# Layer 3's shifted copies in a four-layer convolution kernel: ScalarE copies replaced by DMAs that ScalarE issues

## The chip, the cores and the metric

The kernel runs on one core of a Trainium2 chip. A core has five engines that each work through their own list of instructions in order: PE (TensorE, matrix products), DVE (VectorE), ACT (ScalarE), POOL (GpSimd) and SP (SyncE, which here only issues DMAs). They meet through semaphores. Beside them 16 DMA engines move data between the memories; SP, ACT and POOL can issue DMAs. The metric is the time of one execution on the device in microseconds (us), the median of several runs. The profile is of one execution; its span runs from the first to the last instruction.

## The reference

The input `x` is 16 images of 64 channels of 128 by 128 pixels in float32. Four layers follow each other, each of the form x = x + layer(group_norm(x)):

```python
x = x + _L0_conv_ref(_gn(x), ...)   # channel Gram matrix of the image, then a 1x1 convolution
x = x + _L1_conv_ref(_gn(x))        # |Sobel x| + |Sobel y| in each channel
x = x + _L2_conv_ref(_gn(x), ...)   # shift of some channels by a column, 3x3 convolution, 64 -> 64 channels
x = x + _L3_conv_ref(_gn(x), ...)   # 3x3 convolution, 1x1 convolution, batch norm, leaky ReLU, clip to 0..255
```

`_gn` is a group norm over pairs of channels of one image. The batch norm of layer 3 takes its mean and variance over all 16 images, so the end of layer 3 (normalize, clip, add) can start only when the last image's convolution is done.

## The kernel before, in words

**Tiling.** A tile holds 128 partitions: 64 channels times two rows (or two halves of the image), and along the free axis four pairs of rows of 128 pixels. An image has `NS = 8` chunks of this kind. Products go to PSUM tiles of 512 numbers in each partition.

**The 3x3 convolutions of layers 2 and 3.** Two neighbouring rows of output, `s = 0` and `s = 1`, share rows of input, and a difference of input rows serves in place of some products. `difference(name, n, t)` writes on DVE the difference of two rows into the tile `d2` or `d3`, half `n` of 0 and 1. Each of these tiles is allocated once, 128 partitions by 2 halves by 4 rows by 130 columns, a zero column on either side. `shared(...)` is the product common to both output rows (into a tile `one`), `own(...)` that of one row (into `two`).

**The twins.** For one half of the output channels only one of the two row blocks of the difference is needed, 64 of the 128 partitions. For these the kernel keeps a second tile, `qd2` and `qd3`, called the twin: in one half of its partitions it holds the difference as it is, in the other half the same difference shifted by a column. One product over 128 partitions then serves two columns of the 3x3 kernel (weights `pk`). `own` reads it:

```python
some[o] = [
    (p[cols(o), 0:m], pk, q[:, :, 1:1 + W]),
    (p[cols(o), 0:m, 0:W - 1], wt[:, n, 2, cols(o)], d[:, :, 2:1 + W]),
]
```

`twin(n)` makes the twin of half `n`, in two copies of 64 partitions each. In layer 2 (`Layer2.twin`) POOL issues two DMAs for it. In layer 3 (`Layer3.twin`) ACT makes two copies.

**Order of the work.** The program is a chain of steps (the loop at the end of the kernel), each of four quarters `q = 0..3`. In every step four stages are at work on different images or chunks: Gram (loads `xr`, layer 0's Gram matrix), Front (layer 0's mix and layer 1, from loads `x`; result `u` stored to `x_d`), Layer2 (loads `v` from `x_d`, normalizes them on ACT, result stored to `x_d` again as layer 3's input), and Layer3 (reads layer 2's result from SBUF, writes `y` and stores it to `y_d`). Layer3 runs ten steps behind Layer2, so it is alone in the last steps. Layer 3's part of a step is: at `q = 0` the twin of half 1, the shared product and the product of row 0 (which uses half 0); at `q = 1` the product of row 1 (half 1), the bias `c` on ACT, the normalization of the next chunk, and the stores of the last chunk's `y`; at `q = 2` the sum `y` on DVE and the difference of half 0 for the next step; at `q = 3` the twin of half 0, the difference of half 1, and the squares of `y` on ACT. Layer 2 loads `v` of the chunk after next at `q = 1`, and normalizes the next chunk's `v` there.

The class `InOrder` keeps every engine's instructions in the order in which the program names them. DMAs issued by SP and ACT signal that they have landed by one of eight semaphores, taken in rotation in program order, and a DMA waits until the one that held its semaphore before has landed. POOL's DMAs have eight of their own. Waits between engines, and between a buffer's reader and its next writer, are set by the framework.

**After the last step** the tiles of the earlier stages are used as room for the end: `y_d` and `x_d` are read back, normalized by ACT (ReLU with scale and bias), clipped and added by DVE, and stored.

In the profile nearly all instructions have one line, that of the helper class, so it is read by tiles (`qd<-d`: into a twin from a difference; tile numbers are left out, so `d` and `qd` stand for layers 2 and 3, and `x_d` for the stored results of layers 1 and 2 alike).

Of the kernel before, what the change touches and what calls it, by code (L numbers as in the profile page):

```python
# [15 lines left out]
B, C, H, W = 16, 64, 128, 128  # L16
# [7 lines left out]
CP = 4  # L24
# [20 lines left out]
def single(table, n):  # L45

    for o in range(2):
        planes = [i for m, i, half, _ in table if (m, half) == (n, o)]
        if len(planes) == 1:
            return o, planes[0]  # L50
# [58 lines left out]
def tile_kernel(ctx: ExitStack, tc: tile.TileContext, x, cw_h, w2_t, b2, wbin_t, w1_t, b1, gamma, beta, consts, out):  # L109
    nc = tc.nc  # L110
    pe, dve, act, sp, pool = (InOrder(tc, e) for e in (nc.tensor, nc.vector, nc.scalar, nc.sync, nc.gpsimd))
# [24 lines left out]
    def flat(ap):  # L136
        return ap.rearrange("p j w -> p (j w)")
# [28 lines left out]
    def cols(o):  # L166
        return slice(o * C, (o + 1) * C)
# [568 lines left out]
    class Layer2:  # L736
# [42 lines left out]
        def twin(self, n):  # L779

            d, q = diffs["d2"], twins["d2"]
            _, i = single(TO_SLOTS, n)
            pool.dma_start(flat(q[cols(i), n]), flat(d[cols(i), n]))
            pool.dma_start(
                flat(q[cols(1 - i), n])[:, 1:CP * (W + 2)], flat(d[cols(i), n])[:, 0:CP * (W + 2) - 1]
            )
# [97 lines left out]
    class Layer3:  # L884
# [30 lines left out]
        def twin(self, n):  # L915

            d, q = diffs["d3"], twins["d3"]
            _, i = single(TO_PAIRS, n)
            act.copy(q[cols(i), n, :, 1:1 + W], d[cols(i), n, :, 1:1 + W])
            act.copy(q[cols(1 - i), n, :, 2:2 + W], d[cols(i), n, :, 1:1 + W])  # L920

        def at(self, i, q):
            b = self.b
# [98 lines left out]
    for step in range(starts[2][1] - 2, steps):  # L1022
        for q in range(4):
            for b in range(B):

                i = step - starts[2][1] - NS * b
# [12 lines left out]
            for b in range(1, B):  # L1039
                at, n = pace[b]  # L1040
# [25 lines left out]
            if step >= last_one and q == 2:  # L1066

                n = 3 if step == last_one else 1 if step < last_one + NS - 2 else 0
# [86 lines left out]
```

## Time and profile before

| | |
|---|---|
| median of 3 runs | 2779.62 us (2778.86 to 2781.19) |
| time of the profiled execution, its span | 2778.27 us, 2776.5 us |
| PE busy | 2175.3 us, 78% |
| DVE busy | 2192.0 us, 79% |
| ACT busy | 2112.6 us, 76% |
| POOL busy | 893.2 us, 32% |
| packets of the DMA queue of SP | 613.83 MB, 75.2% of 16 engines' span |
| packets of the DMA queue of POOL | 69.18 MB, 10.2% |

How to read it: busy time is the time in which an engine's instructions execute, without waits and without the issuing of DMAs on SP and ACT. Shares of the whole span are means over stages with different limits. The chunks of all four layers are done in the first 2350 us; the last 426 us are layer 3's end, which moves data. A line of a group gives operation, output and inputs, shape, number, then busy time and mean nanoseconds of one instruction, then the engine's idle time just before these and what ended it. For DMA queues the share is that of the time of 16 engines.

### The profile page before, as it was taken

What the parts mean: (1) busy time and instruction counts of PE and PEld (TensorE: products, weight loads), DVE (VectorE), ACT (ScalarE), POOL (GpSimd) and SP (SyncE); (2) the same over time, 40 slices, a digit from 0 to 9 for tenths busy, and PEclk for the clock granted to TensorE, in tenths of its full rate; (3) what the DMA queues carried; (4) which work ended last, traced back from release to release, by engine and by line L of the source; (5) the groups of instructions that cost most, each with busy time, mean ns of one, the idle gap of its engine ahead of it and who ended that gap; (6) DMA issues with size and microseconds to landing.
All of it is one profiled execution on the core that took longest, in us unless ns stands there. A gap on an engine that the chain in (4) does not pass through costs nothing. (4 is left out here: it accounts for less than half of the span.)

```text
span 2776.5 us, 46105 instructions
## 1 busy us (share of the span) xinstructions
PE 2175.3 (78%) x14804; PEld 886.4 (32%) x14804; DVE 2192.0 (79%) x3623; ACT 2112.6 (76%) x3177; POOL 893.2 (32%) x1350
## 2 busy tenths in 40 slices
PE   6578899999999999999999999999999994000000
PEld 4233433434343434343433342333334641000000
DVE  4999999898989898989899999999996435333332
ACT  4766889898989898989898988999997667333332
POOL 2055434343434343434343344444444300000000
PEclk8689999999999999999999999999999997555555
DMA  8799888988888888888888777878877768999999
GB/s 205 201 229 238 211 216 226 231 215 229 218 227 213 229 221 221 216 230 216 230 218 227 206 188 197 217 202 219 215 199 195 213 196 288 420 420 420 420 420 384
DMA packets 693601, 685.96 MB, mean 247 GB/s; under 512 B 60096, under 2 KB 580448, under 8 KB 693360
## 3 DMA queue, kind: packets, MB, share of 16 engines
q1 hardware_dynamic: 668208, 613.83, 75.2%
q0 software_dynamic: 25152, 69.18, 10.2%
q8 instruction: 119, 1.95, 0.3%
q14 instruction: 122, 1.00, 0.1%
HBM read 346.23 MB, written 268.44 MB: 221 GB/s over the span
## 5 line engine op out<-in xcount | busy, mean ns | idle before, releaser
L73 PE MATMUL two<-d,w 128*64 128x508 f32 (+2 forms) x2560 | 846.8, 588 | 0.0
L73 PE MATMUL two<-d,wi 128*64 128x508 f32 (+3 forms) x1536 | 578.0, 579 | 0.0
L73 POOL DMA_DIRECT2D qd<-d x512 | 270.8, 531 | 903.7 <-DVE d L73 287.4
L73 PE MATMUL two<-qd,pk 128*64 128x512 f32 (+1 forms) x1024 | 519.0, 588 | 13.3 <-DMA qd<-d 12.5
L73 POOL TENSOR_SCALAR edges<-v,co 64x8 f32<-64x8 f32 x512 | 359.9, 703 | 307.7 <-ACT v L73 231.4
L73 DVE TENSOR_TENSOR d<-v 128x512 f32<-128x512 f32 (+1 forms) x512 | 345.6, 678 | 87.6 <-issue 55.5
L73 PE MATMUL one<-v,w 128*64 128x508 f32 (+2 forms) x1600 | 378.6, 599 | 34.8 <-ACT c L73 34.8
L73 PEld LDWEIGHTS two<-d,w 128*64 128x64 f32 x2560 | 263.1, 136 | 314.9 <-issue 278.5
L73 PE MATMUL one<-v,wi 128*64 128x508 f32 (+3 forms) x1536 | 358.5, 599 | 3.1 <-issue 2.6
L73 ACT COPY qd<-d 64x512 f32<-64x512 f32 x512 | 315.4, 616 | 20.8 <-DVE d L73 14.5
L73 DVE SCALAR_TENSOR_TENSOR e<-e 128x1032 f32<-128x1032 f32 (+1 forms) x256 | 312.9, 1222 | 0.0
L73 ACT ACTIVATE xh<-po,co 128x128 f32<-128x128 f32 (+1 forms) x480 | 275.2, 621 | 31.4 <-PE po L73 22.7
L73 POOL TENSOR_SCALAR v<-v,kc 128x9 f32<-128x9 f32 x256 | 234.6, 930 | 12.0
L73 DVE SCALAR_TENSOR_TENSOR y<-two,c 128x1024 f32<-128x1024 f32 x128 | 155.9, 1218 | 102.8 <-ACT v L73 65.4
L73 PEld LDWEIGHTS two<-d,wi 128*64 128x64 f32 x1536 | 175.6, 136 | 186.0 <-issue 169.6
L73 ACT ACTIVATE v<-x,co 128x512 f32<-128x512 f32 (+2 forms) x368 | 234.9, 705 | 0.0
L73 ACT ACTIVATE u<-u 128x1024 f32<-128x1024 f32 x128 | 135.3, 1057 | 106.8 <-DVE u L73 106.4
L73 PE MATMUL po<-x,abd 64*64 64x512 f32 (+1 forms) x1024 | 178.5, 643 | 44.0 <-ACT xh L73 41.0
L73 PEld LDWEIGHTS one<-v,w 128*64 128x64 f32 x1600 | 126.0, 139 | 237.9 <-issue 162.7
L73 PEld LDWEIGHTS two<-qd,pk 128*64 128x64 f32 x1024 | 136.3, 136 | 153.9 <-issue 110.6
L73 PEld LDWEIGHTS one<-v,wi 128*64 128x64 f32 x1536 | 108.9, 138 | 224.1 <-issue 209.0
L73 DVE SCALAR_TENSOR_TENSOR u<-xh 128x1170 f32<-128x1170 f32 x128 | 175.6, 1371 | 5.1 <-ACT xh L73 4.2
(165 smaller groups left out, 3333.9 us busy)
## 6 DMA issues: line engine op xcount, KB each, us to landing
x<-in_x SPq DMA_DIRECT2D x256, 256.0 KB, 4.1
x_d<-u SPq DMA_DIRECT2D x512, 128.0 KB, 3.8
y_d<-y SPq DMA_DIRECT2D x512, 128.0 KB, 4.0
x_d<-x SPq DMA_DIRECT2D x496, 128.0 KB, 2.6
xr<-in_x SPq DMA_DIRECT2D x120, 512.0 KB, 6.4
qd<-d POOLq DMA_DIRECT2D x256, 130.0 KB, 3.1
qd<-d POOLq DMA_DIRECT2D x256, 129.8 KB, 3.9
v<-x_d SPq DMA_DIRECT2D x448, 72.1 KB, 3.3
```

The costliest lines, as they stand in the source:

```text
L73: return self.tc.keep_in_program_order(call(*args, **kwargs))
```

## The change

`Layer3.twin` made its two copies on ACT, each of 64 partitions by 4 rows by 128 columns, within the rows' 130 columns. Now ACT issues two DMAs from SBUF to SBUF for them. They move whole rows of 4 times 130 numbers in each of 64 partitions, zero columns included (the second one number less), so that each partition is one stretch of 2080 or 2076 bytes; the shift by a column is a shift of the stretch by one number. The form is that of `Layer2.twin`, whose DMAs are issued by POOL. Both places that call `twin`, at `q = 3` and at `q = 0`, stay where they are.

```diff
             d, q = diffs["d3"], twins["d3"]
             _, i = single(TO_PAIRS, n)
-            act.copy(q[cols(i), n, :, 1:1 + W], d[cols(i), n, :, 1:1 + W])
-            act.copy(q[cols(1 - i), n, :, 2:2 + W], d[cols(i), n, :, 1:1 + W])
+            act.dma_start(flat(q[cols(i), n]), flat(d[cols(i), n]))
+            act.dma_start(
+                flat(q[cols(1 - i), n])[:, 1:CP * (W + 2)], flat(d[cols(i), n])[:, 0:CP * (W + 2) - 1]
+            )
```

## The prediction

> **What bounds the kernel now.** I read first the busy time in chosen stretches of the span (columns: length, then busy time of PE, its weight loads, DVE, ACT and POOL, the granted clock, the busy share of the 16 DMA engines, GB/s).
>
> ```profile
> core 0: us, PE busy (x) PEld busy (x) DVE busy (x) ACT busy (x) POOL busy (x), PEclk, DMA share, GB/s
> 318.00:2240.00 1922.00, 1871.13 (x12053) 735.99 (x12051) 1742.44 (x2924) 1694.68 (x2660) 775.45 (x1203) 0.99 0.83 215
> ...
> 2240.00:2350.00 110.00, 83.69 (x391) 32.90 (x387) 49.66 (x87) 83.26 (x125) 0.00 (x0) 0.90 0.71 232
> 2350.00:2776.00 426.00, 0.00 (x0) 0.00 (x0) 135.72 (x112) 135.88 (x110) 0.00 (x0) 0.50 1.01 414
> ```
>
> From the first copy of layer 3 (318 us) to 2240 us, PE is busy 97%: it is the bound, 51 us of 1922 are all that a relieved ScalarE could win there. ACT is idle 227 us, DMA engines 17%. The end (426 us) is DMA-bound and not touched. Next the groups of instructions, for prices:
>
> ```profile
> L73 ACT COPY qd<-d 64x512 f32<-64x512 f32 x512 | 315.4, 616 | 20.8 <-DVE d L73 14.5
> L73 PE MATMUL two<-qd,pk 128*64 128x512 f32 (+1 forms) x1024 | 519.0, 588 | 13.3 <-DMA qd<-d 12.5
> ```
>
> PE loses 12.5 us to layer 2's copies, which are DMAs already, and 0.5 us to ScalarE's. Then the DMA issues (engine, count, KB each, median us from issue to landing):
>
> ```profile
> qd<-d POOLq DMA_DIRECT2D x256, 130.0 KB, 3.1
> qd<-d POOLq DMA_DIRECT2D x256, 129.8 KB, 3.9
> v<-x_d SPq DMA_DIRECT2D x448, 72.1 KB, 3.3
> ```
>
> Last the timeline of two steps, SP and then ACT (start, length, engine, operation):
>
> ```profile
> 1213.62 4.69 SPq L73 DMA_DIRECT2D y_d<-y  x4
> 1218.41 2.87 SPq L73 DMA_DIRECT2D v<-x_d  x6
> ...
> 1229.69 3.94 SPq L73 DMA_DIRECT2D y_d<-y  x4
> 1233.74 2.86 SPq L73 DMA_DIRECT2D v<-x_d  x6
> ...
> 1236.70 2.58 SPq L73 DMA_DIRECT2D x_d<-x  x4
> ```
>
> ```profile
> 1219.24 1.24 ACT L73 COPY qd<-d 64x512 f32<-64x512 f32 x2
> ...
> 1222.72 1.25 ACT L73 COPY qd<-d 64x512 f32<-64x512 f32 x2
> ...
> 1228.42 1.35 ACT L73 ACTIVATE v<-v,co 128x1154 f32<-128x1154 f32 x1
> ...
> 1236.05 1.24 ACT L73 COPY qd<-d 64x512 f32<-64x512 f32 x2
> ...
> 1239.54 1.25 ACT L73 COPY qd<-d 64x512 f32<-64x512 f32 x2
> ```
>
> What to see: SP issues nearly without a gap, and it is ahead of ScalarE. In program order the y_d stores and v loads of a step stand beside that step's two pairs of copies, but SP starts them 6 us and more before ACT comes to the copies. This lead keeps v in time: loads issued at 1218.41 to 1221.28 land some 3 us later and are normalized at 1228.42.
>
> [...] No run here yet shows ACT issuing a DMA.
>
> **The change part by part.**
>
> *Removed:* 512 copies by 616 ns, 315 us of ACT.
>
> *Added on ACT:* 512 issues. Nearest rows are SP's: a store of 256 short pieces takes 620 ns (x_d<-x, median), a load of 16 or 32 long rows 419 ns, a full-width load into qd at the end, one long row in each of 128 partitions, 320 ns. The new copies are 64 long rows; I take 350 ns, with 225 ns (the shortest issue of SP's, of a single row, x_d<-w) and 620 ns[...] as ends. A pair then holds ACT 0.70 us where it held it 1.24: 1.08 us less in a step of two pairs, 138 us over 128 steps. By itself this is worth nothing where PE is busy.
>
> *Added on the DMA engines:* 512 times 130 KB, 66.5 MB. Queue 0 (POOL's, mostly the same copies) took 10.2% of 16 engines for 69.2 MB; so 9.8% of 2776 us, or 0.14 of the 1922 us: share 0.83 becomes 0.97 at an unchanged time.
>
> *Longer path to the matmul:* the second copy of a pair is done 1.24 us after ACT starts it; by DMA 0.35 + 0.35 + 3.0 = 3.7 us (3.0 from the rows of 2.5 to 3.9). PE first reads the four pairs above at 1223.42, 1226.20, 1239.44 and 1242.18, so 4.2, 3.5, 3.4 and 2.6 us after ACT's start: in time once, else late by 0.2, 0.3 and 1.1 us, less the 0.54 us by which ACT comes sooner to the second pair of each step. The next subtraction into the same half of d, which must wait until the DMA has read it, comes a step later (17 us) and is covered.
>
> *The new wait, the largest part.* The DMAs of SP and ACT share eight completion semaphores in rotation; each waits until the DMA eight places before it in program order has landed. Before, all eight belonged to SP alone (POOL's DMAs have others). In the built program after, four of some 25 places in a step are ACT's; a y_d store or a v load waits for a copy that ACT issues. In the other direction ACT waits for SP's x_d stores or x loads, which SP issues 10 us and more before ACT comes there (1204 to 1210 for the copies of 1219.24), so that side costs nothing while SP keeps its lead. SP doesn't keep it. Behind its waiting instruction stand the v loads, the x_d stores and the x and xr loads, and for v waits ACT's normalization, with everything behind it on ACT, the next copies included.
>
> The loop, with the timeline's numbers (landing 3.0, store freed by the pair's first copy at +3.4, last loads by the second pair at +3.7):
> Step 1: y_d waits until 1219.24 + 3.4 = 1222.6 instead of 1213.62. Stores and loads take 4.8 and 2.9, end 1230.3, land 1233.3; the normalization stood at 1228.42: 4.8 us late. All of ACT moves by this.
> Step 2: SP needs 8.4 us for its other issues (1221.28 to 1229.69) and is free at 1238.7, but the pair of 1236.05 now starts at 1240.9 and frees the store at 1244.3; loads end at 1251.2, land 1254.2; normalization at 1246.56 + 4.8 = 1251.4: a further 2.8.
> The five steps after it, worked in the same way, give 1.6, 4.9, 3.6, 3.7 and 2.9. Mean of the seven: 24.3 / 7 = 3.5 us a step.
>
> Not all of it remains. ACT does 1.1 us less, and its idle time, 227 us in 118 steps or 1.9 a step, takes up some; with half of it 3.5 - 1.1 - 0.95 = 1.5 us a step (ends: 0.5 with all of it, 2.4 with none). 83 such steps are 125 us. In the last 35 steps before the tail Front's loads and the Gram loads have run out and SP has a third less to issue: I take half, 26 us. The late pair lies within the same delay, since PE is then waiting anyway.
>
> *The tail:* in the last nine or so steps layer 3 is alone, a step takes 7.8 us, and PE's first read follows the copy's end by 0.1 us (2272.32, 2272.39): there 3.7 in place of 1.24 is paid in full, 2.45 x 9 = 22 us.
>
> Sum: 2776.5 + 125 + 26 + 22 = 2949.5 us span, and 1.8 us around it as in the profiled execution (2778.3, against the median 2779.6 of three): 2951; I say 2950.
>
> **The rivals.**
> A. *The DMA engines join in:* at a share of 0.97 landings lengthen. If each grows by a fifth, 0.7 us, the loop has three of them, 2.1 us; with half of that taken up, 1 us by 118 more: 3070. For it: the engines are already the fullest shared resource after PE. Against: a longer run lowers the share (0.97 x 2776 / 2950 = 0.91).
> B. *Only the late pair counts:* SP catches up[...]. Then PE waits about 0.5 us in each of 118 steps, plus the tail: 59 + 22, 2860. Against: SP has no gap in which to catch up.
> C. *Faster:* SP's hold-up stays within v's slack. The chain of waits gives PE 41.0 us waiting for xh and 34.8 us for c from ACT; half of that goes with a lighter ACT: 2740. It decides where the seven latenesses are overstated by their mean, 3.5 us: that needs DMAs that land in a quarter of a microsecond, or a SP that issues half as long. Against it the DMA rows, none of which has a median under 1.9 us.
> D. *It doesn't relieve ACT:* at 620 ns an issue ACT gains nothing, and the rest remains: 2780 if the waits are hidden too.
>
> **How the numbers follow.** Forecast 0.60, A 0.15, B 0.13, C 0.08, D 0.04. Slower by over 0.2%: 0.88; faster 0.08; the same 0.04 (0.2% is about what three runs from 2778.9 to 2781.2 can tell from no change). The forecast's own range, with 0.9 to 2.1 us a step over 101 full-step equivalents, is 2890 to 3010; with B below and A above it the range becomes 2810 to 3080, which leaves out C, D and the far part of A.
>
> **What would show it.** Right: the 616 ns copies are gone, ACT issues 512 DMAs of 0.3 to 0.6 us landing in 3 to 4 us; on SP y_d and v start after ACT's copies, not 6 us before; ACT's normalization of v waits for v<-x_d, which is in no wait of ACT's before; PE's busy share between 318 us and the tail falls from 97% to about 91%; a tail step takes about 10 us. Wrong: SP's lead unchanged; PE waiting for qd alone (B); PE as busy as before. The number fails first if ACT's idle time takes up more of the lateness than half, or if landings lengthen.

## The result, and the profile after

The changed kernel takes 2937.39 us (median of 4 runs, 2930.95 to 2941.92) against 2780.40 us of the kernel before beside it: a ratio of 1.0563 (95% interval 1.0542 to 1.0584), 157 us more. The forecast was 2950. The profiled execution took 2936.55 us; its span is 2934.8 us, 158.3 us longer than before.

Where in the program the time was lost can be read from PE's products by tile. Layer 2's products into `two` have the weights `wi`, layer 3's the weights `w`; the last one of each tells when layer 2 and layer 3 were done. Columns: operation and count, shortest/median/longest duration in ns, first and last start in us, forms. First the kernel before, then after:

```profile
L73 PE MATMUL two<-d,w x2560: 481/588/1054, 172.4 to 2323.2; 128*64 128x508 f32 x156, 128*64 128x512 f32 x36, 128*64 128x381 f32 x5
L73 PE MATMUL two<-d,wi x1536: 481/588/1106, 171.5 to 2244.5; 128*64 128x508 f32 x111, 128*64 128x512 f32 x65, 128*64 128x381 f32 x16
```

```profile
L73 PE MATMUL two<-d,w x2560: 481/588/1110, 172.4 to 2481.4; 128*64 128x508 f32 x154, 128*64 128x512 f32 x38, 128*64 128x381 f32 x5
L73 PE MATMUL two<-d,wi x1536: 481/588/1110, 171.5 to 2364.5; 128*64 128x508 f32 x112, 128*64 128x512 f32 x64, 128*64 128x381 f32 x16
```

Layer 2's last product comes 120.0 us later (2364.5 against 2244.5). From there to layer 3's last product it takes 116.9 us instead of 78.7, 38.2 more. From that to the end of the span it is 453.4 and 453.3: the end is untouched. So 120 us went in the part with layer 2, called the stage below, and 38 in layer 3's tail.

The busy time in the stage (columns as in the prediction):

```profile
core 0: us, PE busy (x) PEld busy (x) DVE busy (x) ACT busy (x) POOL busy (x), PEclk, DMA share, GB/s
318.00:2240.00 1922.00, 1792.43 (x11474) 669.68 (x11472) 1704.93 (x2829) 1343.99 (x2102) 699.76 (x1121) 0.99 0.90 233
```

PE is busy 93% of the same stretch, in which it now gets through 11474 recorded products instead of 12053. ACT's busy time fell by 351 us, and PE gained nothing from it. The DMA engines' share rose from 0.83 to 0.90.

The groups of instructions after (busy us and mean ns | idle time before them, and what ended most of it):

```profile
L73 PE MATMUL two<-qd,pk 128*64 128x512 f32 (+1 forms) x1024 | 531.7, 601 | 117.3 <-DMA qd<-d 111.6
L73 ACT ACTIVATE v<-v,co 128x1154 f32<-128x1154 f32 x128 | 172.8, 1350 | 431.0 <-DMA v<-x_d 375.5
```

PE waits 111.6 us for twins where it waited 12.5. The larger wait is the second line's, ACT's normalization for layer 2's `v`; ACT is not the bound, so its wait costs time only by what comes late behind it, the twins among it. That line before had no idle time ahead of it at all:

```profile
L73 ACT ACTIVATE v<-v,co 128x1154 f32<-128x1154 f32 x128 | 172.0, 1344 | 0.0
```

SP's own waits after (us, times, longest); SP had no wait for `qd<-d` before:

```profile
SPq L73 <- DMA qd<-d: 160.3, 109, 6.5
```

The DMA issues after (count, KB each, median us to landing), then the queue that ACT's DMAs use (packets, MB, share of 16 engines):

```profile
qd<-d POOLq DMA_DIRECT2D x256, 130.0 KB, 3.6
qd<-d ACTq DMA_DIRECT2D x256, 130.0 KB, 3.0
...
qd<-d ACTq DMA_DIRECT2D x256, 129.8 KB, 3.8
v<-x_d SPq DMA_DIRECT2D x448, 72.1 KB, 3.5
```

```profile
q10 hardware_dynamic: 40960, 68.12, 8.7%
```

The new copies land in 3.0 and 3.8 us, where 3.0 was taken for both. (The profile tells the landing of only a part of the DMAs of SP and ACT, here of 99 of ACT's 512.) Of the older transfers some land later than before (`y_d` 4.8 us for 4.0, POOL's twins 3.6 for 3.1), some sooner (`xr` 6.1 for 6.4). Last, a step in the timeline after, of SP and then of ACT:

```profile
1321.27 0.56 SPq L73 DMA_DIRECT2D xr<-in_x  x1
1323.23 2.74 SPq L73 DMA_DIRECT2D y_d<-y  x4
1326.08 5.19 SPq L73 DMA_DIRECT2D v<-x_d  x6
```

```profile
1320.40 0.47 ACTq L73 DMA_DIRECT2D qd<-d  x1
...
1320.91 0.61 ACTq L73 DMA_DIRECT2D qd<-d  x1
...
1325.00 1.22 ACTq L73 DMA_DIRECT2D qd<-d  x2
...
1334.43 1.35 ACT L73 ACTIVATE v<-v,co 128x1154 f32<-128x1154 f32 x1 [1.52 <-DMA v<-x_d]
```

SP stands still from 1321.83 to 1323.23, 1.4 us that the trace puts down to `qd<-d`, until 2.8 us after ACT's first pair was issued; and the loads of `v`, spread to 1331.27, end only 3.2 us before the normalization. The lead that SP had is gone in this step. In the trace the first store of `y_d` waits for the semaphore (number 116) with which the first copy of ACT's first pair signals, and starts 17 ns after the copy landed. Until then SP issues nothing else: its loads of `v` stand behind the stores and begin at 1326.08. Two of the six loads wait in the same way for the pair of 1325.00 and start 16 and 17 ns after its copies landed.

### The profile page after: what moved, and what is told of

Read it like the earlier page. It is cut to its first block, busy times and chain, and to the rows that moved or that the text cites. A ratio compares the mean times of both kernels' runs of the same rounds, so it can differ in the third digit from the quotient of the medians.

```text
span 2934.8 us, 46626 instructions
## 1 busy us (share of the span) xinstructions
PE 2226.0 (76%) x14804; PEld 897.3 (31%) x14804; DVE 2200.8 (75%) x3623; ACT 1793.2 (61%) x2665; POOL 854.8 (29%) x1350
## 5 line engine op out<-in xcount | busy, mean ns | idle before, releaser
L73 PE MATMUL two<-d,w 128*64 128x508 f32 (+2 forms) x2560 | 898.3, 605 | 0.0
L73 PE MATMUL two<-qd,pk 128*64 128x512 f32 (+1 forms) x1024 | 531.7, 601 | 117.3 <-DMA qd<-d 111.6
L73 POOL TENSOR_SCALAR edges<-v,co 64x8 f32<-64x8 f32 x512 | 342.7, 669 | 596.8 <-ACT v L73 290.5
L73 ACT ACTIVATE v<-v,co 128x1154 f32<-128x1154 f32 x128 | 172.8, 1350 | 431.0 <-DMA v<-x_d 375.5
L73 PE MATMUL one<-v,w 128*64 128x508 f32 (+2 forms) x1600 | 374.5, 590 | 39.7 <-ACT c L73 39.1
L73 DVE SCALAR_TENSOR_TENSOR u<-xh,co,u 128x1024 f32<-128x1024 f32 x128 | 164.7, 1287 | 85.6 <-ACT u L73 85.3
L73 POOL TENSOR_SCALAR v<-v,kc 128x9 f32<-128x9 f32 x256 | 213.3, 846 | 12.0
L73 ACT ACTIVATE junk<-y 128x1024 bf16<-128x1024 f32 x128 | 134.8, 1053 | 83.2 <-PE two L73 38.1
```

What stands on the lines that cost most here:

```text
L73: return self.tc.keep_in_program_order(call(*args, **kwargs))
```

## The experiments

Two theories were set against each other. **Shared semaphores:** SP waits, at the eight semaphores it shares with ACT, for ACT's copies to land; `v` comes late, and ACT with it. (In the trace after, SP's 3241 DMAs and ACT's 512 signal by the same eight, GpSimd's 526 by eight others.) **Late pair:** PE waits for twins that are made in 3 to 4 us instead of 1.2. A third, the **load** of 66.5 MB more on the DMA engines, goes with both.

All runs, with the split as above (from each profiled execution; the stage's loss is against 2244.5, the tail's against 78.7):

| run | median us | ratio, 95% interval | stage | tail |
|---|---|---|---|---|
| the change | 2937.39 | 1.0563 (1.0542 to 1.0584) | +120.0 | +38.2 |
| e1 GpSimd asks | 2906.00 | 1.0451 (1.0435 to 1.0466) | +84.2 | +46.7 |
| e2 tiny DMAs beside, ScalarE | 2803.48 | 1.0079 (1.0064 to 1.0094) | +25.8 | +1.4 |
| e3 full DMAs beside, GpSimd | 2795.72 | 1.0050 (1.0029 to 1.0070) | +39.9* | 0.0 |
| e4 full DMAs beside, ScalarE | 2863.41 | 1.0296 (1.0281 to 1.0311) | +78.8 | +6.6 |
| e5 sooner, ScalarE asks | 2946.10 | 1.0598 (1.0582 to 1.0614) | +133.0 | +34.1 |
| e6 sooner, GpSimd asks | 2870.32 | 1.0340 (1.0306 to 1.0374) | +51.6 | +38.6 |
| e7 only half 1 by DMA | 2827.56 | 1.0172 (1.0157 to 1.0187) | +44.0 | +5.2 |
| e8 only half 0 by DMA | 2834.85 | 1.0200 (1.0183 to 1.0217) | +29.8 | +27.6 |
| e9 the tail by copies | 2914.85 | 1.0491 (1.0470 to 1.0513) | +129.4 | +6.1 |
| e10 sooner, GpSimd, tail by copies | 2836.86 | 1.0212 (1.0179 to 1.0245) | +49.8 | +4.6 |
| e11 copies named sooner | 2800.61 | 1.0079 (1.0062 to 1.0096) | +20.8 | -0.3 |
| e12 tiny, ScalarE, and full, GpSimd | 2902.39 | 1.0442 (1.0416 to 1.0467) | +112.7 | +9.2 |

\* e3's profiled execution (2817.90) is the longest of its seven (2787.30 to 2817.90); its median is 15.5 us above that of the kernel before beside it, and this is what is used. The four executions of e6 span 23 us, those of e10 21, those of the other runs 14 or less, so differences of that size in the last two columns, which are from one execution each, say nothing.

### e1: the same DMAs, asked for by GpSimd

GpSimd's DMAs have eight semaphores of their own, so nothing of SP's waits for these copies. The places stay.

```diff
-            act.dma_start(flat(q[cols(i), n]), flat(d[cols(i), n]))
-            act.dma_start(
+            pool.dma_start(flat(q[cols(i), n]), flat(d[cols(i), n]))
+            pool.dma_start(
```

> The same twin DMAs, issued by POOL in place of ACT; POOL's DMAs have completion semaphores of their own, bytes and matmuls stay as in the changed kernel. Theory (SP is held back by the semaphores that it shares with ACT's DMAs): SP has its lead again, ACT's waits for v<-x_d fall from 375 us to under 50, the time is 2790 to 2870 (the late pair and the tail remain). Rival, late twins at PE: 2900 to 2940, as changed. Rival, the DMA engines' load: 2900 to 2940 too, since the bytes are the same.

Measured: 2906. The groups of this run:

```profile
L73 PE MATMUL two<-qd,pk 128*64 128x512 f32 (+1 forms) x1024 | 538.3, 608 | 138.7 <-DMA qd<-d 138.1
...
L73 ACT ACTIVATE v<-v,co 128x1154 f32<-128x1154 f32 x128 | 171.7, 1341 | 18.9 <-DMA x_d<-x 15.1 <-DMA v<-x_d 3.8
```

ACT's wait for `v` falls from 375.5 to 3.8 us. SP has its lead again: loads issued from 1295.20 to 1298.07 are normalized at 1308.70. The bytes and the reader are the same, so in the changed kernel it is the shared semaphores that make `v` late. But only 36 of the stage's 120 us came back, because PE now waits longer for twins (138.1 us; from 318 to 2240 us they are all for layer 3's, by the products that follow). The time lies above the 2790 to 2870 that was expected if the shared semaphores were the main loss. Without them, late twins and the added bytes still cost 84 us. A part of this may be GpSimd's order, which was not separated: it asks for half 1's pair together with a pair of layer 2, four DMAs in one row, and that row starts only when DVE has a difference ready:

```profile
1318.95 2.05 POOL L73 DMA_DIRECT2D qd<-d  x4 [3.29 <-DVE d L73]
```

### e2, e3, e4, e12: the DMAs without a reader

In these the copies of the kernel before stay, so that no product waits for a DMA of layer 3. Beside each pair, DMAs go from the difference into memory that nobody reads. In e2 ScalarE asks for two tiny ones (64 rows of 16 numbers), in e3 GpSimd for two of full size, in e4 ScalarE for these. In e12 both are there, ScalarE's tiny and GpSimd's full ones.

```diff
+    spare = [dram.tile([P, CP * (W + 2)], F32, name=f"spare{n}") for n in range(2)]
...
             act.copy(q[cols(1 - i), n, :, 2:2 + W], d[cols(i), n, :, 1:1 + W])
+            act.dma_start(spare[n][cols(i)], flat(d[cols(i), n]))
+            act.dma_start(
+                spare[n][cols(1 - i), 1:CP * (W + 2)], flat(d[cols(i), n])[:, 0:CP * (W + 2) - 1]
+            )
```

That is e4; e3 has `pool` in place of `act`, e2 sends `d[cols(i), n, 0, 0:16]` alone, e12 adds this to e3.

> ACT's copies as before; beside each, ACT issues a DMA of 64 rows of 16 numbers from the difference to a spare place in DRAM that nobody reads. Almost no bytes, no product waits for it; only the places in the rotation of semaphores, and ACT's issues, are those of the changed kernel. Theory: most of the loss comes back, 2850 to 2930, ACT waits over 150 us for v<-x_d. Rival, late twins at PE: 2780 to 2800. Rival, the DMA engines' load: 2780 to 2800.

> ACT's copies as before; beside each, POOL issues a DMA with the changed kernel's number of bytes (64 rows of 2080 or 2076) to a spare place in DRAM that nobody reads. Bytes without shared semaphores and without a product that waits. Theory: 2780 to 2810. Rival, late twins: 2780 to 2800. Rival, the DMA engines' load: 2880 to 2940.

> ACT's copies as before; beside each, ACT issues a DMA with the changed kernel's number of bytes to a spare place in DRAM that nobody reads. Shared semaphores and bytes, but no product that waits, and ACT's copies are back (315 us of ACT). Theory: 2890 to 2980, ACT waits over 250 us for v<-x_d. Rival, late twins at PE: 2780 to 2800. Rival, the DMA engines' load: 2880 to 2940, with POOL as issuer as well as with ACT.

> ScalarE's copies stay; beside each pair ScalarE asks for two tiny DMAs (64 rows of 16 numbers), which share the semaphores' rotation, and GpSimd for two of full size, which have their own; no reader waits for any of the four. Tiny ones alone cost 22 us, full-size ones on their own semaphores alone 15, but full-size ones in the shared rotation 83. If the two costs simply add: 2810 to 2825, and the rest of the 83 belongs to full-size transfers that themselves hold a shared semaphore. If the load on the DMA engines makes the shared rotation dearer whoever moves the bytes (SP's own landings get longer, so its lead gets shorter): 2845 to 2870, with ScalarE waiting 120 us or more for v.

Measured, median against the median of the kernel before beside it: e2 +23.3 us, e3 +15.5, e4 +83.2, e12 +123.8. The waits of ACT for `v` and of SP for these DMAs, in e2, e4 and e12:

```profile
ACT v L73 <- DMA v<-x_d: 68.2, 31, 5.5
...
SPq L73 <- DMA spare<-d: 180.8, 111, 6.1
```

```profile
ACT v L73 <- DMA v<-x_d: 159.0, 58, 7.3
...
SPq L73 <- DMA spare<-d: 94.2, 77, 6.2
```

```profile
ACT v L73 <- DMA v<-x_d: 215.1, 77, 9.4
...
SPq L73 <- DMA tiny<-d: 115.9, 85, 5.8
```

e2 missed the shared-semaphore theory's 2850 to 2930 by far: SP waits at least as long as in the changed kernel (180.8 us), tiny DMAs land no sooner (3.5 us), and yet `v` is late for 68 us only and the kernel loses 23. SP's waiting was mostly made good again in e2, at a DMA share of 0.84 in the stage. `v` is late in e3 as well, whose DMAs share no semaphore with SP: at a share of 0.90 ACT waits 66.7 us for it in the profiled (slowest) execution. With the load added by another queue, e12 loses 124, over five times as much and three times the sum of the parts (23.3 + 15.5). It also lies above the 2845 to 2870 that was expected for that case. e4 fell short of its range, 2890 to 2980 with over 250 us of waiting for `v`. So the shared semaphores can cost nearly as much as the stage lost, 112.7 of 120 us, with no product waiting for a DMA of layer 3; but only together with the load. What tips it isn't visible in one number: landings differ little (`v` 3.1 us in e2, 3.5 in e3 and e4, 3.7 in e12; `y_d` 3.3, 4.2, 4.2, 4.2). Why e12 is 39 us above e4, with the same bytes and the same number of DMAs in the rotation, stays open; GpSimd has 512 more issues there (542 ns each) which its own work stands behind. In e2, e4 and e12 ScalarE does copies and issues both, more than in either kernel, and so has less room to make up for a late `v`; what the semaphores and the load cost in the changed kernel may be less than e4 and e12 lose.

### e5 and e6: both pairs asked for a quarter sooner

Half 0's pair moves from `q = 3` to `q = 2`, behind its difference, half 1's from the next step's `q = 0` to `q = 3`. ScalarE asks in e5, GpSimd in e6.

```diff
                     difference("d3", 0, self.v[i + 1])
+                    self.twin(0)
...
-                    self.twin(0)
                     difference("d3", 1, self.v[i + 1])
+                    self.twin(1)
```

> The changed kernel with both pairs asked for a quarter of a step sooner, right behind the subtraction that they copy (half 0 at q=2, half 1 at q=3); ACT issues them. If late pairs at PE are the larger part of the loss: PE's waits for qd<-d fall from 112 us to under 50 and the time to 2830 to 2880, which leaves the part of the shared semaphores and the bytes (the run with bytes beside, asked for by ACT, lost 83 us). If the shared semaphores are the larger part: 2900 to 2950, ACT still waits over 250 us for v<-x_d.

> The same, issued by POOL: sooner and with semaphores of its own. Late pairs as the larger part: 2785 to 2830, since neither is left and the bytes alone cost 15 us; the tail's steps stay longer by some 3 us each. If what POOL's version loses is something else (its own order, the load on the DMA engines): 2880 to 2910 as with POOL asking at the old places.

Measured: e5 2946, e6 2870. PE's waits in e5 between 318 and 2240 us:

```profile
PE one L73 <- ACT c L73: 126.6, 66, 4.7
PE two L73 <- DMA qd<-d: 6.9, 5, 2.1
```

In the changed kernel the same stretch has 39.1 us for `c` and 79.8 for twins. In e5 the late pair is all but gone there, and the time is no better: ACT, still held up by `v` (299.7 us) and with SP waiting 192.7 us for pairs, now gives PE its `c` late. Even without the 20 us that the order alone costs (e11 below), e5's stage loses some 112 of the 120 us, so taking away the late pair brought almost nothing back. Only with both causes eased, in e6, does the stage's loss halve. e6 lies in neither of its ranges; `v` is still late there, by 99.4 us in all, though SP shares no semaphore with these DMAs, at a DMA share of 0.94 in the stage.

### e11: the order of e5 and e6, with copies

```diff
-            act.dma_start(flat(q[cols(i), n]), flat(d[cols(i), n]))
...
+            act.copy(q[cols(i), n, :, 1:1 + W], d[cols(i), n, :, 1:1 + W])
+            act.copy(q[cols(1 - i), n, :, 2:2 + W], d[cols(i), n, :, 1:1 + W])
```

The diff is against e5.

> No DMA: the kernel before, with ScalarE's copies of both pairs named a quarter sooner, which is the order that the two runs with sooner requests had. It tells whether that order alone costs or gains, so whether those two runs may be read against the kernel before. TensorE waited 0.5 us for ScalarE's twins before, so nothing is to be won by it: theory 2775 to 2800 (ScalarE's squares and c come later by a pair, and TensorE waited 35 us for c). If order alone made the difference in the sooner runs, it is above 2840.

Measured: 2800.61. The order alone costs 20 us where ScalarE does the copies, and PE's wait for `c` in the stage grows from 34.8 to 67.7 us, so a part of e5's late `c` may be the order's (in e6 its place on ScalarE is empty, so that cost need not apply there). It can't explain the sooner runs' 2870 and 2946.

### e7 and e8: one half by DMA, the other by copies

```diff
+            if n == 1:
                 act.dma_start(flat(q[cols(i), n]), flat(d[cols(i), n]))
...
+            else:
+                act.copy(q[cols(i), n, :, 1:1 + W], d[cols(i), n, :, 1:1 + W])
+                act.copy(q[cols(1 - i), n, :, 2:2 + W], d[cols(i), n, :, 1:1 + W])
```

The diff is against the changed kernel, without regard to indentation. e7 is this one, e8 has `n == 0`.

> Only half 1's pair (asked for at q=0, read at q=1) by ACT's DMAs, half 0's pair by ACT's copies. Late pairs: half 1 has the smaller margin, so most of the loss is here, 2860 to 2910, PE waits over 60 us for qd<-d. Shared semaphores: half the places in the rotation, 2840 to 2870, as with half 0.

> Only half 0's pair (asked for at q=3, read at the next q=0) by ACT's DMAs, half 1's by copies. Late pairs: larger margin, 2800 to 2840. Shared semaphores: 2840 to 2870, as with half 1.

Measured: 48 and 56 us, together 104 of 157; in the stage 44 + 30 of 120. Both are less than was expected of the shared semaphores, and e7 much less than was expected of late pairs. Half of the issues and bytes cost less than half: the loss grows faster than its causes, as in e2, e3 and e12. The tail, though, is half 0's. PE's waits from 2290 to 2380 us in e8, then in e7:

```profile
PE two L73 <- DMA qd<-d: 27.2, 9, 5.4
```

```profile
PE two L73 <- DMA qd<-d: 3.0, 8, 1.8
```

### e9 and e10: the tail made by copies

The last image's pairs, whose steps all come after layer 2, are copies again; in e9 from the change (the diff below, without regard to indentation), in e10 from e6.

```diff
+            if self.b < B - 1:
                 act.dma_start(flat(q[cols(i), n]), flat(d[cols(i), n]))
...
+            else:
+                act.copy(q[cols(i), n, :, 1:1 + W], d[cols(i), n, :, 1:1 + W])
+                act.copy(q[cols(1 - i), n, :, 2:2 + W], d[cols(i), n, :, 1:1 + W])
```

> The change, but the pairs of the last image, all of whose steps come after layer 2 has ended (nine steps), are made by ScalarE's copies as before. Prediction's sum: the tail is 22 us of 171, so about 2915. With the tail's steps of 10.5 to 12 us in the changed kernel's trace against 7.8 before, 9 x (11.5 - 7.8) = 33 us: about 2904, and a tail step of about 8 us again. If the tail's steps were long for another reason (the squares and c behind the issues), less than 10 us comes back: 2927 or more.

> Twins asked for by GpSimd a quarter sooner, so with no shared semaphore and the least waiting of TensorE so far (2870), and the last image's pairs by ScalarE's copies. If the tail is worth 22 to 33 us here too: 2837 to 2848. What is then left above 2780, some 60 us, belongs to the stage before the tail alone: late twins still (TensorE waited 77 us for them in all, of which the tail's share now goes) and the DMA engines' load of 0.94. If the tail is worth nothing here because the sooner request had already hidden it: 2865 or more.

Measured: 22.5 us less than the change (2914.85), 33.5 less than e6 (2836.86). In both the tail itself becomes 32 to 34 us shorter; e9's stage lost 9 more than the change's in the one execution profiled, which is within what executions differ by. e10 is the fastest form in which all copies of the stage are DMAs, and is still 2.1% slower than the kernel before. No run beat that one.

## Why the prediction was right, and where its steps were off

**The bound.** Right. ACT's busy time in the stage fell by 351 us without any gain; rival C (2740) needed a relieved ACT to count. Of the two waits that it counted on, the 41.0 us for `xh` all lie before 318 us, where no copy of layer 3 has begun.

**The price of an issue.** Too low, but it mattered less than the forecast thought. The tile's view after has this line (shortest/median/longest ns):

```profile
L73 ACTq DMA_DIRECT2D qd<-d x512: 467/494/1872, 315.9 to 2474.3; - x171
```

494 ns against the 350 taken, inside the stated ends of 225 and 620. But issues mostly run beside ACT's instructions: of 258 us of them in the stage 219 lie over an instruction that executes (summed from their starts and ends; an example is below). So ACT was relieved by more than the 1.1 us a step of the sum, and it was of no use.

**The DMA engines.** The added queue took 8.7% of 2935 us, 255 us of 16 engines, against 272 worked out; their share in the stage is 0.90 against 0.91 expected at 2950. But the load was weighed as a rival of its own (A, longer landings, 3070), and the forecast left it out. e2 shows that this was the wrong division: without the bytes the rotation costs 0.2 us a step (26 us in 118), with them 0.7 in e4 and 1.0 in e12.

**The new wait.** Its mechanism is shown: ACT waits 375.5 us for `v` after, 0 before, and 3.8 when the copies stay DMAs but leave SP's semaphores (e1). Its size was worked out as 1.5 us for each of 83 full steps and 26 us for the rest, 151 us in all; the stage lost 120, 1.0 us a step, and by e1 only 36 of them come back without this wait. The raw loop's 3.5 us a step rested on a misreading: SP "issues nearly without a gap" holds for the two steps shown, not for the stage. SP's waits from 318 to 2240 us, before, then after:

```profile
SPq L73 <- DVE d L73: 84.7, 54, 5.6
SPq L73 <- DVE u L73: 36.2, 35, 5.2
```

```profile
SPq L73 <- DMA qd<-d: 124.7, 96, 6.5
SPq L73 <- DMA x<-in_x: 52.1, 58, 2.3
SPq L73 <- DMA xr<-in_x: 43.0, 27, 3.4
...
SPq L73 <- DVE d L73: 10.1, 21, 0.9
SPq L73 <- DVE u L73: 9.4, 19, 0.9
```

Before, SP waited 121 us for these two kinds of tile from DVE. After, most of this is gone, 20 us are left: SP comes later, and finds them ready. Over the whole span it is 60 us in e2 against 169 before, so e2 makes good some 109 of the 181 us that SP waits for the tiny DMAs; that SP has no gap in which to catch up, the argument against rival B, was wrong. The same lines show a cost that the loop lacks: SP waits 95 us for its own loads of `x` and `xr`, where it waited 7 (6.1 for `xr`). With four more DMAs a step in the rotation a semaphore comes round sooner, while its last DMA is still on its way; over the whole span the two are 117 us after, 28 before, and 31 in e1, without ACT's places. These errors have opposite signs, and no run separates them.

**The late pair.** "Lies within the same delay, since PE is then waiting anyway": supported, and in a stronger sense than meant. Without the late pair the loss of the stage is 79 (e4) to 113 us (e12), without the shared semaphores 84 (e1), with both 120: the causes overlap and are not added. For the same reason neither undoing brings back its own size, and rival B, which gave the late pair 59 us in the stage, was too low for it taken alone as well, as far as e1 tells. In the path of 0.35 + 0.35 + 3.0 us the second 0.35 is counted twice, since the view's landings count from the start of an issue; with the 0.49 and 3.8 measured it is 4.3.

**The tail.** The step was right in kind and too small: 22 us predicted, 38.2 lost. PE's busy time from layer 2's last product to layer 3's, before and after (columns as in the prediction), and its wait after:

```profile
2244.50:2323.20 78.70, 78.20 (x350) 29.32 (x347) 25.35 (x51) 57.99 (x98) 0.00 (x0) 1.00 0.64 195
```

```profile
2364.50:2481.40 116.90, 90.41 (x350) 35.44 (x347) 25.36 (x51) 35.00 (x60) 0.00 (x0) 0.87 0.66 193
PE two L73 <- DMA qd<-d: 26.5, 9, 4.4
```

Nine pauses take 26.5 us, 2.9 each against the 2.45 worked out. The rest the sum left out: the same 350 recorded products take 12.2 us longer, at a mean granted clock of 0.87 instead of 1.00. In e9, where these pauses are nearly gone (PE waits 0.9 us for ScalarE's copies in the whole run), the tail is back to 84.8 us. No run changed the clock alone.

**The total.** 120 + 38 measured against 151 + 22: the sum was within 0.5%, but by a stage 31 too long and a tail 16 too short. That it came so near is in part luck: errors of both signs stand in the stage's term, and the wait called the largest part gives back only 31 us when it alone is taken away (e1: 2906).

## What to carry to other kernels

Before a copy is handed to a DMA, look at whose completion semaphores it will share: a queue that ran far ahead is tied by them to the engine that now issues beside it, and what it loaded early may come late (here ACT waited 375.5 us for `v` with the tie, 3.8 without it). Price the DMA engines' load together with that tie, for each alone was small here (16 and 23 us) and both together were not (124), in runs in which ScalarE kept its copies besides. Read how far ahead a queue is, and what it waits for, over the whole stage and not in two steps. And where two causes are each enough for the loss, taking away one brings back only what the other leaves (here 31 of 157 us in e1, nothing in e5): undo both, and undo each, before one is called the cause; a stretch in which one layer runs alone is summed separately, at the full latency (here 2.9 us in each of nine pauses).

## What was not expected of the hardware

**An issue runs beside an instruction of its own engine.** In the timeline of ACT after, a DMA is issued while the square ahead of it still executes:

```profile
1305.83 1.05 ACT L73 ACTIVATE junk<-y 128x1024 bf16<-128x1024 f32 x1
1306.63 0.47 ACTq L73 DMA_DIRECT2D qd<-d  x1
```

The square runs from 1305.83 to 1306.88, the issue starts at 1306.63. So the 494 ns of an issue are not simply added to ACT's instructions. In e12, where ScalarE has its copies too, an issue of 0.45 us at 1307.39 lies wholly within an instruction that runs from 1307.31 to 1308.35.

**A tiny DMA is asked for no faster and lands no sooner.** Both into the same kind of place in DRAM, in 64 rows: 4.0 KB took 482 ns to issue (e2, medians) and landed in 3.5 us there, in 3.7 in e12; 130 KB took 472 ns and landed in 3.5 or 4.1 us (the first and the second of a pair, e4), at a DMA share of 0.84, 0.88 and 0.89. Between these two sizes a semaphore is held about as long.

**Products were slow after pauses of under 3 us, but the length of a pause alone did not decide it.** In the tail eight of PE's nine pauses were 2.43 to 2.85 us long, and after seven of the eight some products took about 1.06 us in place of 0.59. But of two pauses of 2.85 us one was followed by slow products at once and the other only 2.8 us later, and a pause of 2.77 us was followed by none:

```profile
2394.33 1.09 PE L73 MATMUL two<-qd,pk 128*64 128x512 f32 x1 [2.85 <-DMA qd<-d]
...
2464.14 0.61 PE L73 MATMUL two<-qd,pk 128*64 128x512 f32 x1 [2.85 <-DMA qd<-d]
...
2466.98 1.08 PE L73 MATMUL two<-qd,pk 128*64 128x512 f32 x1
```

What decides after which of them products are slow, and when, stays open.
